# Layer 1 of a two-layer attention kernel: x1 loaded a second time in runs of 32 channels and turned by VectorE block transposes, in place of TensorE transposes

## The chip, the core and the metric

The kernel runs on one core of one Trainium2 chip. A core has five engines that run side by side and wait for each other through semaphores: TensorE (matrix products, PE in the profile; its weight loads are shown apart as PEld), VectorE (DVE), ScalarE (ACT), GpSimd (POOL) and SyncE (SP), which here only issues DMA transfers. Sixteen DMA engines move data between the device's main memory (HBM) and the core's on-chip memory (SBUF, 128 partitions). TensorE writes its results to PSUM, a small memory of its own, from which ScalarE and VectorE fetch them.

The metric is the device time of the whole program in microseconds (us), the median of several runs.

## What is computed

The input x has the shape (1, 128, 256, 256): 128 rows of 256 positions with 256 channels. Two layers follow each other. Each normalizes its input by groups of channels over the whole tensor, applies attention to every row of 256 positions, and adds the result to its input. Layer 0 has 8 heads, a bias from a pair tensor z and a gate. Layer 1, which the change concerns, has 4 heads of 64 channels and lets each position see only those at most 16 away. Cut to what matters:

```python
def _L1_conv_ref(x, w_in, b_in, w_out, b_out, band):
    x2 = x.reshape(B * T, F, C)
    qkv = x2 @ w_in.T + b_in
    q, k, v = jnp.split(qkv, 3, axis=-1)
    q, k, v = (heads(q), heads(k), heads(v))
    scores = jnp.einsum('bhid,bhjd->bhij', q, k) / jnp.sqrt(jnp.asarray(D, x.dtype))
    keep = jnp.abs(i - j) <= band
    scores = jnp.where(keep, scores, -jnp.inf)
    attn = jax.nn.softmax(scores, axis=-1)
    out = jnp.einsum('bhij,bhjd->bhid', attn, v)
    out = out.transpose(0, 2, 1, 3).reshape(B * T, F, C)
    return out @ w_out.T + b_out

x = x + _L0_conv_ref(_gn(x), ...)
x = x + _L1_conv_ref(_gn(x), ...)
```

All data is fp32.

## The kernel before

`fast_kernel` runs layer 0 over 64 pairs of rows and writes its result, x1, to HBM: sixteen tensors of 8 rows each (GB = 8, that is 4 pairs), stored when they are full (L1430). The sums for layer 1's normalization are collected along the way in `st1`. `general_kernel` stands behind a branch at the end and is taken only when a range check has failed.

**A pair in layer 1.** The class `Pair1` holds the work on two rows (512 positions). Its constructor allocates `xt` (positions on the partitions: 128 partitions, 4 blocks of positions, 256 channels; 4 buffers) and issues on SP the load of 512 KB from x1 (L1717), in contiguous runs of 1 KB. The projections need the channels on the partitions. So `transpose(k)`, for each half k of the channels, turns four blocks of 128x128 on TensorE into one PSUM buffer (L1730), and `centre(k)` moves that buffer to `xgT` on ScalarE, subtracting the channel's mean (L1733). After the second half GpSimd adds the output bias to `xt` in place (L1735), so that the residual needs one addition less later. `turn(k)` is the two together.

`project` makes q and k (four products a pair, evicted by ScalarE, L1747), `values` makes v (L1758, L1762), `scores` the products of q and k within the band (L1772), which ScalarE exponentiates (L1780) and GpSimd multiplies with a mask of the band in two instructions, e*bw (L1782). `apply` multiplies with v and sums the weights (L1800). `combine` brings the halves together on VectorE: sum (L1812), reciprocal (L1813), sum (L1814), product (L1816), and stores the reciprocals on SP (L1819). `out_row` projects back (L1831), VectorE adds `xt` (L1835, `yo`), and SP stores two rows (L1843).

**PSUM.** Transposes, projections, values and out_row take turns in two buffers named `mm`. A product can begin only when the one two places before it has been evicted. Scores, apply's results and its sums have buffers of their own, single ones.

**Order.** Within `manual_schedule` each engine's instructions follow the order of the program. The loop over p (L1884) is a pipeline over pairs: `now` does its scores and first apply, `was`, the pair before, its second apply and its output, `nxt` its projections, and `nn`, two pairs ahead, its load (at the top of the stage), and `turn(0)` and `turn(1)`. On TensorE the two groups of four transposes stand just ahead of `scores(1)` and, at the end of a stage, ahead of the next stage's `scores(0)`. On VectorE a stage has: `yo` of row 0, combine of row 1, combine of row 0, `yo` of row 1, and then, while there are any, one range check of three instructions (L958 to L960). There are 15 such checks, on `eb`, on the input mask and on sums read back from HBM; those of layer 0 come in stages 1 to 13, two more near the end.

**Entry.** Layer 1 begins with pairs 0 and 1: their loads, the transposes of pair 0 on TensorE, then `norm1`, which makes mean and scale from `st1` (VectorE L1682 copies the means, TensorE averages them, L1683 and L1691, VectorE and GpSimd follow) and multiplies the scale into `w_in` on VectorE (L1701). Then pair 0 is centred and projected, and pair 1 turned.

Of the kernel before, what the change touches and what calls it, by code (L numbers as in the profile page):

```python
# [9 lines left out]
F32 = mybir.dt.float32  # L10
AF = mybir.ActivationFunctionType
# [5 lines left out]
P = 128  # L17
# [4 lines left out]
def bcast(ap, axis, n):  # L22

    ap = ap.unsqueeze(axis)
    shape = list(ap.shape)
    shape[axis] = n
    return ap.broadcast_to(shape)
# [746 lines left out]
def fast_kernel(  # L774
# [25 lines left out]
    nc = tc.nc  # L800
    S, I, C = x.shape
# [6 lines left out]
    NB = I // P  # L808
    KC = C // P
    NP = S // 2  # L810
    N2 = 2 * I
# [7 lines left out]
    ident = const.tile([P, P], F32, name="ident")  # L819
# [89 lines left out]
    def rows(ap, s0, n):  # L909
        return ap[s0 : s0 + n].rearrange("s (b p) c -> p (s b) c", p=P)  # L910
# [20 lines left out]
    for a in range(KC):  # L931
        for h in range(H1):
            n = P // H1
# [5 lines left out]
    for h in range(H1):  # L939
        n = P // H1  # L940
# [257 lines left out]
    GB = min(8, S)  # L1198
    HQ = P // D0
    NT = 2 * NB  # L1200
    x1 = [dram.tile([GB, I, C], F32, name=f"x1_{j}") for j in range(S // GB)]
# [16 lines left out]
    class Pair:  # L1218


        def __init__(self, p):
            self.p = p
            self.oT = {}
            self.xt = la.tile([P, NT, C], F32, name="xt", tag="xt", bufs=5)
            nc.sync.dma_start(
                self.xt.rearrange("p (s b) c -> p s (b c)", b=NB),
                x[2 * p : 2 * p + 2].rearrange("s (p b) c -> p s (b c)", b=NB),
            )


        def centre(self):
            self.xg = la.tile([P, NT, C], F32, name="xg", tag="xg", bufs=2)
            nc.gpsimd.tensor_tensor(self.xg, self.xt, bcast(M0, 1, NT), ALU.subtract)
# [33 lines left out]
        def turn(self, pss=None):  # L1267
            self.xgT = la.tile([P, KC, N2], F32, name="xgT", tag="xgT", bufs=2)
            if pss is None:
                ps = ps_s.tile([P, KC, N2], F32, name="ps_x", tag="s")  # L1270
                pss = [ps[:, k, :] for k in range(KC)]
            for k in range(KC):
                for t in range(NT):
                    nc.tensor.transpose(  # L1274
                        pss[k][:, t * P : (t + 1) * P], self.xg[:, t, k * P : (k + 1) * P], ident
                    )
            for k in range(KC):
                nc.scalar.copy(self.xgT[:, k, :], pss[k])
# [201 lines left out]
    now = nxt = nn = None  # L1480
# [47 lines left out]
    behind, nx, n = None, 0, 0  # L1528
# [41 lines left out]
    with tc.manual_schedule():  # L1570
        old = was = Nobody()
        es = nn3 = None
        for p in range(NP):
# [49 lines left out]
            old, was, now, nxt, nn = was, now, nxt, nn, nn3  # L1623
# [21 lines left out]
    def q0(k):  # L1645
        return min(max(k * KB - BAND, 0), I - W)

    def half(k):
        return slice((k % 2) * KB, (k % 2 + 1) * KB)
# [9 lines left out]
            )  # L1659

    DH = P // H1
    LATE = 8
    rsum1 = dram.tile([NP, H1, 2, I], F32, name="rsum1")
    with tc.tile_pool(name="l1", bufs=2) as sb, tc.tile_pool(
        name="l1s", bufs=4
    ) as sm, tc.tile_pool(name="ps1_mm", bufs=2, space=PSUM) as ps_mm, tc.tile_pool(
        name="ps1_s", bufs=1, space=PSUM
    ) as ps_s, tc.tile_pool(name="ps1_o", bufs=1, space=PSUM) as ps_o:

        def mm1(name):  # L1670
            return ps_mm.tile([P, 512], F32, name=name, tag="mm")

        nM1 = const.tile([P, KC], F32, name="nM1")
# [36 lines left out]
        class Pair1:  # L1710


            def __init__(self, p):
                self.p = p
                s0 = 2 * p
                self.xt = sb.tile([P, 2 * NB, C], F32, name="xt1", tag="xt", bufs=4)
                nc.sync.dma_start(self.xt, rows(x1[s0 // GB], s0 % GB, 2))  # L1717
                self.es, self.oT = {}, {}

            def turn(self, k):  # L1720
                self.transpose(k)
                self.centre(k)

            def transpose(self, k):
                if k == 0:
                    self.xgT = sb.tile([P, KC, N2], F32, name="xgT1", tag="xgT")
                    self.ps_x = {}
                ps = self.ps_x[k] = mm1("ps_x1")
                for t in range(2 * NB):
                    nc.tensor.transpose(ps[:, t * P : (t + 1) * P], self.xt[:, t, k * P : (k + 1) * P], ident)  # L1730

            def centre(self, k):
                nc.scalar.activation(self.xgT[:, k, :], self.ps_x[k], AF.Identity, bias=nM1[:, k : k + 1])  # L1733
                if k == KC - 1:
                    nc.gpsimd.tensor_tensor(self.xt, self.xt, bcast(bout_r, 1, 2 * NB), ALU.add)  # L1735

# [50 lines left out]
            def apply(self, r):  # L1787
# [3 lines left out]
                for a in range(3):  # L1791
                    for j in range(NK // 2):
                        for h in range(H1):
                            for k in (2 * j, 2 * j + 1):
                                at = slice(h * DH, (h + 1) * DH)
                                n = k % 2
                                to = o_eo[n][at, a, q0(k) : q0(k) + W] if a < 2 else su_eo[n][at, q0(k) : q0(k) + W]
                                w = (self.v[half(k), r, j, h * D1 + a * DH : h * D1 + (a + 1) * DH] if a < 2
                                     else ones[half(k), :DH])
                                nc.tensor.matmul(  # L1800
# [3 lines left out]
            def combine(self, r):  # L1804
# [12 lines left out]
                self.oT[r] = oT  # L1817
                if r == 1 and self.p < NP - LATE:
                    nc.sync.dma_start(rsum1[self.p].rearrange("q r i -> q (r i)"), rv[0:P:DH].rearrange("q r i -> q (r i)"))  # L1819
                elif r == 1 and self.p < NP - 1:  # L1820
# [24 lines left out]
        def pair1(p):  # L1845
            return Pair1(p) if p < NP else Nobody()
# [5 lines left out]
        def check_all(src, lo, hi):  # L1852
            for i in range(0, src.shape[1], 512):
                n = min(512, src.shape[1] - i)
                checks.append(lambda i=i, n=n: check(src[:, i : i + n], lo, hi, sm))

        def load_sums(src, name):
            t = sb.tile([P, src.shape[0] // P], F32, name=name, tag=name, bufs=1)
            nc.sync.dma_start(t, src.rearrange("(a b) -> a b", a=P))
            check_all(t, 1e-16, 1e8)  # L1860

        with tc.manual_schedule():
            now, nxt = pair1(0), pair1(1)
            for k in range(KC):
                now.transpose(k)
            norm1()
            for k in range(KC):
                now.centre(k)
            for m in range(KC):
                now.project("qT", m)  # L1870
                now.project("kT", m)
            for r in range(2):
                now.values(r)
            for k in range(KC):
                nxt.turn(k)
        check_all(eb.rearrange("p h b i -> p (h b i)"), math.exp(-20.0), math.exp(20.0))
        mask_t = sb.tile([S, I], F32, name="mask_all", bufs=1)
        nc.sync.dma_start(mask_t, mask)
# [3 lines left out]
        with tc.manual_schedule():  # L1882
            was = Nobody()
            for p in range(NP - 1):  # L1884
                nn = pair1(p + 2)
                if p == NP - LATE + 2:
                    load_sums(rsum1[: NP - LATE].rearrange("n q r i -> (n q r i)"), "sums1")

                now.scores(0)
                was.apply(1)  # L1890
                was.out_row(0)
                was.combine(1)
                nxt.project("qT", 0)
                nxt.project("kT", 0)
                nxt.project("qT", 1)
                nn.turn(0)

                now.scores(1)
                now.apply(0)
                now.combine(0)  # L1900
                nxt.project("kT", 1)
                if p < NP - 2:
                    nxt.values(0)
                    nxt.values(1)
                was.out_row(1)
                nn.turn(1)
                if checks and p > 0:
                    checks.pop(0)()
                was, now, nxt = now, nxt, nn
            assert not checks  # L1910

            now.scores(0)
            was.apply(1)
            was.combine(1)
            now.values(0)
            was.out_row(0)
            now.scores(1)
            now.values(1)
            now.apply(0)
            now.combine(0)  # L1920
            was.out_row(1)
            now.apply(1)
            now.combine(1)
            now.out_row(0)
            now.out_row(1)
# [3 lines left out]
        ps = mm1("ok_ps")  # L1929
# [4 lines left out]
@with_exitstack  # L1934
def mixer_kernel(ctx, tc, *args):

    nc = tc.nc
    keep = ctx.enter_context(tc.tile_pool(name="verdict", bufs=1))
    verdict = keep.tile([1, 1], mybir.dt.int32, name="verdict")
    fast_kernel(tc, *args, verdict)  # L1940
    again = nc.values_load(verdict[0:1, 0:1], min_val=0, max_val=1)
    with tc.If(again > 0):
        general_kernel(tc, *args)
# [53 lines left out]
```

## Time and profile before

| What | Value |
|---|---|
| Median of 3 runs | 3363.17 us (3362.63 to 3363.67) |
| Profiled execution, from first to last instruction | 3356.3 us |
| Mean granted TensorE clock | 0.985 of full |
| Layer 1's transposes on TensorE (L1730) | 512, 128x128 fp32, busy 77.6 us |
| ScalarE centring (L1733) | 128, mean 683 ns |
| GpSimd bias addition (L1735) | 64, mean 2374 ns |
| VectorE `yo` (L1835) | 128, mean 690 ns |
| VectorE reciprocal of 128x256 (L1813) | 128, mean 1753 ns |
| DMA in layer 1, 2500 to 2600 us | engines busy 0.18 of the time, 55 GB/s |

The profile is of one execution, whose span is 3356.3 us; the runs' times are a few us longer because they count what lies around the first and last instruction too. Durations below are from that execution. The busy time of TensorE is modelled: its matrix instructions overlap, and a record's duration reaches from its start to the end of its pipeline. What an instruction really occupies is better read from start to start. Layer 1 begins at about 2095 us and lasts to the end.

### The profile page before, as it was taken

How to read it: one execution, taken by the hardware profiler on the slowest of the kernel's cores; microseconds unless marked ns; L12 is line 12 of the kernel's file. 1: busy time of each engine (PE TensorE's matmuls, PEld its weight loads, DVE VectorE, ACT ScalarE, POOL GpSimd, SP SyncE). 2: the span in 40 equal slices, each digit the busy share in tenths (PEclk: the TensorE clock that was granted, in tenths of full speed). 3: DMA queues.
4: the chain of work that ended last, by engine and by line, in shares of the span. 5: the costliest groups of instructions: out<-in, count | busy, mean ns of one | idle time of the engine just before them, and what ended most of it. 6: DMA issues, size and time to landing. Idle time of an engine off the chain costs nothing.

```text
span 3356.3 us, 81416 instructions
## 1 busy us (share of the span) xinstructions
PE 3210.8 (96%) x35168; PEld 2039.6 (61%) x35168; DVE 2021.7 (60%) x3115; ACT 1461.1 (44%) x2121; POOL 1961.9 (58%) x1375
## 2 busy tenths in 40 slices
PE   5389999999999999999999998999999999999998
PEld 3255555555555555555555555667777677677676
DVE  7955666666666666666666666466544444443456
ACT  2264444444444444444444443344444444444443
POOL 2378787777777787887777774333333333333332
PEclk8699999999999999999999999999999999999999
DMA  9941212221222222122212221111211211112111
GB/s 350 369 135 43 74 49 74 74 74 49 74 74 57 58 71 68 49 74 74 74 49 74 74 65 47 64 53 53 65 53 53 65 53 58 60 53 61 57 58 53
DMA packets 198640, 262.39 MB, mean 78 GB/s; under 512 B 46240, under 2 KB 147488, under 8 KB 197120
## 3 DMA queue, kind: packets, MB, share of 16 engines
q1 hardware_dynamic: 193200, 254.19, 24.7%
q8 instruction: 279, 4.57, 0.6%
q10 hardware_dynamic: 5072, 2.90, 0.3%
q14 instruction: 89, 0.73, 0.1%
HBM read 188.30 MB, written 68.75 MB: 77 GB/s over the span
## 4 chain that ended last, share of the span: by engine, by line
PE 91%; DVE 4%; DMA 3%; ACT 1%; POOL 1%; issue 1%; SPq 0%; ACTq 0%; POOLq 0%; DVEq 0%
PE ps_p L1296 20%; PE ps_p L1743 14%; PE ps_sc L1330 8%; PE ps_y L1831 7%; PE ps_ov L1362 7%; PE ps_v L1758 7%; PE ps_y L1417 6%; PE ps_v L1311 6%; PE ps_o L1800 3%; PE ps_sc L1772 3%; PE ps_su L1370 3%; PE ps_x L1274 2%; PE ps_x L1730 2%; PE ps_su L1800 1%; DVE st L1178 1%; DVE zst L1103 1%
## 5 line engine op out<-in xcount | busy, mean ns | idle before, releaser
L1351 POOL TENSOR_TENSOR eboth<-e 128x512 f32<-128x512 f32 x512 | 639.9, 1271 | 391.7 <-DVE e L1346 389.7
L1346 DVE TENSOR_TENSOR e<-ps_sc,eb 128x1024 f32<-128x1024 f32 x512 | 603.2, 1220 | 304.9 <-ACT ps_sc L1337 304.8
L1337 ACT ACTIVATE ps_sc<-ps_sc 128x1024 f32<-128x1024 f32 x512 | 492.8, 1006 | 509.2 <-PE ps_sc L1330 509.2
L1782 POOL TENSOR_TENSOR e<-e,bw 128x384 f32<-128x384 f32 x256 | 258.7, 1031 | 444.3 <-ACT e L1780 444.3
L1743 PE MATMUL ps_p<-xgT,w_in 128*128 128x512 f32 x1024 | 469.2, 601 | 3.7 <-DVE w_in L1701 3.7
L1735 POOL TENSOR_TENSOR xt<-xt,bout_r 128x1024 f32<-128x1024 f32 x64 | 152.0, 2374 | 379.0 <-PE ps_x L1730 379.0
L1835 DVE TENSOR_TENSOR yo<-ps_y,xt 128x512 f32<-128x512 f32 x128 | 88.3, 690 | 379.1 <-PE ps_y L1831 379.1
L1743 PEld LDWEIGHTS ps_p<-xgT,w_in 128*128 128x128 f32 x1024 | 188.9, 190 | 203.0 <-issue 170.9
L1330 PE MATMUL ps_sc<-qT,kT 32*128 32x256 f32 x4096 | 293.3, 400 | 2.0 <-ACT kT L1300 2.0
L1296 PE MATMUL ps_p<-xnT,wq 128*128 128x512 f32 x512 | 266.0, 631 | 3.5 <-POOL xnT L1283 2.9
L1831 PE MATMUL ps_y<-w_out,oT 128*128 128x256 f32 x1024 | 249.1, 386 | 2.6 <-DVE oT L1816 2.6
L1362 PE MATMUL ps_ov<-e,v 128*32 128x256 f32 x4096 | 247.7, 382 | 0.0
L1417 PEld LDWEIGHTS ps_y<-wo,oT 128*128 128x128 f32 x1024 | 194.3, 190 | 82.4 <-issue 59.3
L1417 PE MATMUL ps_y<-wo,oT 128*128 128x256 f32 x1024 | 242.0, 379 | 2.0 <-POOL oT L1407 1.2
L1330 PEld LDWEIGHTS ps_sc<-qT,kT 32*128 32x128 f32 x4096 | 184.9, 184 | 94.4 <-issue 83.6
L1311 PE MATMUL ps_v<-wv,xnT 128*128 128x256 f32 x1024 | 242.2, 379 | 0.0
L1296 PE MATMUL ps_p<-xnT,wk 128*128 128x512 f32 x512 | 240.6, 592 | 0.0
L1296 PE MATMUL ps_p<-xgT,wg 128*128 128x512 f32 x512 | 236.8, 605 | 0.0
L1758 PE MATMUL ps_v<-w_in,xgT 128*128 128x256 f32 x1024 | 231.8, 379 | 0.0
L1813 DVE RECIPROCAL rv<-odd 128x256 f32<-128x256 f32 x128 | 224.4, 1753 | 4.4
L1758 PEld LDWEIGHTS ps_v<-w_in,xgT 128*128 128x128 f32 x1024 | 194.4, 190 | 53.5 <-issue 30.1
L1311 PEld LDWEIGHTS ps_v<-wv,xnT 128*128 128x128 f32 x1024 | 189.6, 190 | 50.8 <-issue 31.0
(170 smaller groups left out, 4958.8 us busy)
## 6 DMA issues: line engine op xcount, KB each, us to landing
xa<-in_x_dram SPq DMA_DIRECT2D x8, 4096.0 KB
xt<-in_x_dram SPq DMA_DIRECT2D x64, 512.0 KB
x<-xo SPq DMA_DIRECT2D x16, 2048.0 KB
xt<-x SPq DMA_DIRECT2D x64, 512.0 KB
rvb<-rsum SPq DMA_DIRECT2D x252, 128.0 KB
out_dram<-yo SPq DMA_DIRECT2D x63, 512.0 KB
zt<-in_z_dram SPq DMA_DIRECT2D x15, 2048.0 KB
rs_r<-rs_d SPq DMA_DIRECT2D x63, 256.0 KB
```

What stands on the lines that cost most here:

```text
L1296: nc.tensor.matmul(ps, w[:, k, m * P : (m + 1) * P], getattr(self, src)[:, k, :], start=(k == 0), stop=(k == KC - 1),)
L1311: nc.tensor.matmul(self.ps_v[:, b * C : (b + 1) * C], self.xnT[:, k, t * P : (t + 1) * P], wv[:, k, :], start=(k == 0), stop=(k == KC - 1),)
L1330: nc.tensor.matmul(self.pss[q // 2][:, q % 2, b, :], self.kT[rs, c, r * I + b * P : r * I + (b + 1) * P], self.qT[rs, c, r * I : (r + 1) * I],
L1337: nc.scalar.activation(self.pss[a], self.pss[a], AF.Exp)
L1346: nc.vector.tensor_tensor(e, pss[a], eb[:, h : h + 2], ALU.mult)
L1351: nc.gpsimd.tensor_tensor(t, es[a][:, :, 0, :], es[a][:, :, 1, :], ALU.add)
L1362: nc.tensor.matmul(ov[q * D0 : (q + 1) * D0, c, :], self.v[:, r, b, h * D0 : (h + 1) * D0], es[q // 2][:, q % 2, b, :], start=(b == 0), st ...
L1417: nc.tensor.matmul(self.ps_y[:, b * C : (b + 1) * C], self.oT[r][:, k, b * P : (b + 1) * P], wo[:, k, :], start=(k == 0), stop=(k == KC - 1),)
L1743: nc.tensor.matmul(ps, w_in[:, k, n * C + m * P : n * C + (m + 1) * P], self.xgT[:, k, :], start=(k == 0), stop=(k == KC - 1),)
L1758: nc.tensor.matmul(ps[:, b * C : (b + 1) * C], self.xgT[:, k, t * P : (t + 1) * P], w_in[:, k, 2 * C : 3 * C], start=(k == 0), stop=(k == ...
L1782: nc.gpsimd.tensor_tensor(e[:, q], e[:, q], bcast(bw.rearrange("p b w -> p (b w)"), 1, KC), ALU.mult)
L1831: nc.tensor.matmul(ps[:, b * C : (b + 1) * C], self.oT[r][:, k, b * P : (b + 1) * P], w_out[:, k, :], start=(k == 0), stop=(k == KC - 1),)
```

## The change

Each pair is loaded twice. The old load into `xt` stays, for the residual, with 6 buffers instead of 4. A second load brings the same rows into `xs` (3 buffers) in four DMAs, one for each block j of 32 partitions: the partition of block j is the position within its run of 32 positions, and along the free dimension lie, for each half k of the channels and each run of 32 positions, 32 contiguous channels (128 bytes), channels k*128 + j*32 to k*128 + j*32 + 31. One VectorE instruction then transposes all 32x32 blocks of `xs` into `xT`, which has the channels on the partitions. `centre` reads `xT` instead of PSUM; `transpose` on TensorE is gone. The load now goes out three pairs ahead (`n3`), and `turn` stands at the end of a stage, after `yo` of row 1 and ahead of the range check; `centre(0)` and `centre(1)` of the pair after it stand where the two halves of `turn` stood. At the entry both pairs' `turn` stand ahead of `norm1`.

```diff
+    QB = 32
...
-                self.xt = sb.tile([P, 2 * NB, C], F32, name="xt1", tag="xt", bufs=4)
+                two = x1[s0 // GB][s0 % GB : s0 % GB + 2]
+                self.xs = sb.tile([P, KC, N2], F32, name="xs1", tag="xs", bufs=3)
+                for j in range(P // QB):
+                    nc.sync.dma_start(
+                        self.xs[j * QB : (j + 1) * QB].rearrange("b k (i a) -> b k i a", a=QB),
+                        two.rearrange("s (i b) (k j a) -> j b k (s i) a", b=QB, k=KC, a=QB)[j],
+                    )
+                self.xt = sb.tile([P, 2 * NB, C], F32, name="xt1", tag="xt", bufs=6)
                 nc.sync.dma_start(self.xt, rows(x1[s0 // GB], s0 % GB, 2))
                 self.es, self.oT = {}, {}
 
-            def turn(self, k):
-                self.transpose(k)
-                self.centre(k)
-
-            def transpose(self, k):
+            def turn(self):
+                self.xT = sb.tile([P, KC, N2], F32, name="xT1", tag="xT")
+                nc.vector.transpose(self.xT.rearrange("p k n -> p (k n)"), self.xs.rearrange("p k n -> p (k n)"))
+
+            def centre(self, k):
                 if k == 0:
                     self.xgT = sb.tile([P, KC, N2], F32, name="xgT1", tag="xgT")
-                    self.ps_x = {}
-                ps = self.ps_x[k] = mm1("ps_x1")
-                for t in range(2 * NB):
-                    nc.tensor.transpose(ps[:, t * P : (t + 1) * P], self.xt[:, t, k * P : (k + 1) * P], ident)
-
-            def centre(self, k):
-                nc.scalar.activation(self.xgT[:, k, :], self.ps_x[k], AF.Identity, bias=nM1[:, k : k + 1])
+                nc.scalar.activation(self.xgT[:, k, :], self.xT[:, k, :], AF.Identity, bias=nM1[:, k : k + 1])
                 if k == KC - 1:
                     nc.gpsimd.tensor_tensor(self.xt, self.xt, bcast(bout_r, 1, 2 * NB), ALU.add)
...
             now, nxt = pair1(0), pair1(1)
-            for k in range(KC):
-                now.transpose(k)
+            now.turn()
+            nxt.turn()
             norm1()
...
             for k in range(KC):
-                nxt.turn(k)
+                nxt.centre(k)
...
             for p in range(NP - 1):
-                nn = pair1(p + 2)
+                nn = pair1(p + 2) if p == 0 else n3
+                n3 = pair1(p + 3)
+                if p == 0:
+                    nn.turn()
...
                 nxt.project("qT", 1)
-                nn.turn(0)
+                nn.centre(0)
...
                 was.out_row(1)
-                nn.turn(1)
+                nn.centre(1)
+                n3.turn()
                 if checks and p > 0:
                     checks.pop(0)()
```

## The prediction

> **What bounds the kernel now.** I read the page's busy shares first, then layer 1 in the chain of waits, then one steady pair in the timeline, then the places where the change adds something: VectorE beside the checks, the entry into layer 1, and the DMA of short runs.
>
> The page: TensorE is the only engine near its limit.
>
> ```profile
> PE 3210.8 (96%) x35168; PEld 2039.6 (61%) x35168; DVE 2021.7 (60%) x3115; ACT 1461.1 (44%) x2121; POOL 1961.9 (58%) x1375
> ...
> PE 91%; DVE 4%; DMA 3%; ACT 1%; POOL 1%; issue 1%; SPq 0%; ACTq 0%; POOLq 0%; DVEq 0%
> ```
>
> The chain within layer 1 (start us, us, what): one pair every 2622.98 - 2603.71 = 19.27 us, TensorE without a hole, and the transposes (ps_x) in it.
>
> ```profile
> 2603.71 5.15 PE ps_p L1743 x12
> 2608.86 0.44 PE ps_x L1730 x4
> 2609.30 0.82 PE ps_sc L1772 x32
> ...
> 2622.98 2.15 PE ps_p L1743 x5
> ```
>
> The timeline of that pair (start us, us, engine, line, what, and the idle time before it) shows both groups of four transposes with their neighbours, and what VectorE does from one eviction `yo` to the next: nothing, for 3.84 us.
>
> ```profile
> 2608.70 0.60 PE L1730 MATMUL ps_x<-ident,xt 128*128 128x128 f32 x4
> 2609.22 0.70 PEld L1772 LDWEIGHTS ps_sc<-qT,kT 64*64 64x64 f32 x32 [0.17 <-issue]
> 2618.34 0.60 PE L1730 MATMUL ps_x<-ident,xt 128*128 128x128 f32 x4
> 2618.54 0.69 DVE L1835 TENSOR_TENSOR yo<-ps_y,xt 128x512 f32<-128x512 f32 x1 [3.21 <-PE ps_y L1831]
> 2618.87 0.89 PE L1772 MATMUL ps_sc<-qT,kT 64*64 64x96 f32 x32
> 2623.07 0.69 DVE L1835 TENSOR_TENSOR yo<-ps_y,xt 128x512 f32<-128x512 f32 x1 [3.84 <-PE ps_y L1831]
> ```
>
> In 15 of the pairs a range check (L958 has 8 on eb, 1 on the mask, 6 on sums) fills just that gap. It delays the second `yo` so far that the weight load of the next projection waits for it; there the period is 19.30 us (2218.04 to 2237.34 in the chain), so the gap is used up to within 0.03 us.
>
> ```profile
> 2174.99 0.69 DVE L1835 TENSOR_TENSOR yo<-ps_y,xt 128x512 f32<-128x512 f32 x1 [3.21 <-PE ps_y L1831]
> 2175.47 2.38 POOL L1735 TENSOR_TENSOR xt<-xt,bout_r 128x1024 f32<-128x1024 f32 x1 [5.93 <-PE ps_x L1730]
> 2175.60 2.54 DVE L958 TENSOR_SCALAR chk<-eb 128x512 f32<-128x512 f32 x1
> 2178.17 1.37 DVE L959 SCALAR_TENSOR_TENSOR chk<-eb,chk 128x512 f32<-128x512 f32 x1
> 2180.18 0.68 DVE L1835 TENSOR_TENSOR yo<-ps_y,xt 128x512 f32<-128x512 f32 x1
> 2180.91 0.30 PEld L1743 LDWEIGHTS ps_p<-xgT,w_in 128*128 128x128 f32 x2 [0.59 <-DVE yo L1835]
> ```
>
> The entry into layer 1: SP and VectorE are both let go by the last store of layer 0 at 2095.4; TensorE, in order, first waits for xt and transposes it, and only then does the mean (L1683), whose input is ready at 2095.8.
>
> ```profile
> 2095.44 0.93 SPq L1717 DMA_DIRECT2D xt<-x  x2
> 2095.48 0.29 DVE L1682 COPY gn_each<-st 128x256 f32<-128x256 f32 x1 [2.92 <-DMA x<-xo]
> 2099.54 1.94 PE L1730 MATMUL ps_x<-ident,xt 128*128 128x128 f32 x8 [11.98 <-issue]
> 2101.27 1.06 PE L1683 MATMUL ps_gn<-gn_each,avg 128*128 128x256 f32 x2
> ```
>
> **What the Trainium skill says.** "VectorE: DVE Perf Modes", The three transpose paths: VectorE turns 32x32 blocks only, which is why the load must place the blocks; no run shows it yet. "DMA: Bandwidth & Descriptors", Specifications: transfers under 512 B miss line rate; the new runs have 128 B. The trace agrees in direction only: 1 KB packets take about 51 ns (DMA view from 2600 to 2640 us: 2311 packets in 18.4% of 16 engines), while the 4-byte packets of `rs_d` take some 11 ns each (DMA view from 1016 to 1020 us: 512 packets, 32 an engine, within about 0.4 us). "SBUF — State Buffer", Who interferes with whom: VectorE and GpSimd share a port pair as an exclusive lock, taken by tensor_scalar and by instructions with two SBUF inputs. The trace agrees: L958 takes 2.54 us and ends just after POOL L1735, but 0.42 us in the same shape (`chk<-rv`) with GpSimd idle.
>
> **The change part by part.**
>
> Removed on TensorE. Start to start, the transposes hold it from 2608.70 to 2609.23 and from 2618.34 to 2618.87: 0.53 us twice, 1.06 us a pair. (The chain, which counts by ends, gives 0.44 twice; that is the lower bound.) Pairs 1 to 63 have them in the stream: 63 x 1.06 = 66.8 us. Pair 0 belongs to the entry, below. What is late next: nothing. With the transposes gone the two PSUM buffers `mm` rotate over eight users instead of ten, still even, and apply, out_row and project keep their 2 to 8 us of distance from what VectorE and ScalarE deliver.
>
> Added on VectorE: one transpose of 128x1024 per pair. The trace has none. Nearest row: tensor_tensor of 128x1024 (L1346) at 1.22 us, and "Vector Engine (DVE) Microarchitecture Reference", The reshape front-end and per-opcode configuration, states one element per cycle per lane. I take 1.22. Lower bound 0.7 (two per cycle); upper bound the rate of the reciprocal, 1753 ns for 256, that is 7.0 us. It stands right behind the second row's `yo`, with behind it in the queue (checks aside) the other row's `yo`. That one is wanted 0.53 us earlier than before: 4.53 - 0.53 = 4.0 us after the first, and the projection tolerates about 0.63 more. 0.61 + 1.22 = 1.83 fits: cost nothing, up to a transpose of 4.0 us.
>
> With a check behind it. Transpose ends at 1.83; GpSimd no longer waits for TensorE with the bias add (it moves forward behind the e*bw products, and may hold up one L1816 by 0.8 us, which has 5 us), but its two e*bw products of 0.98 us then begin at about 1.7. L958 waits for the first (to 2.7), L959 for the second, and `yo` starts at about 5.0 against a limit of 4.63: 0.37 us lost. If L958 comes first, nothing is lost; if the check costs its full 4.6 us, 1.8 us. I take 0.35 x 15 = 5 us, range 0 to 27.
>
> ScalarE reads xT in SBUF instead of PSUM: same count, 0.68 us each, with the input two stages old; no cost.
>
> DMA. Per pair four loads of 32 partitions, each 32 x 32 runs of 128 B: 4096 runs, 256 an engine when the 32 partitions spread over 16. From 11 ns at 4 B and 51 at 1 KB a straight line gives 16 ns at 128 B: 4.1 us a pair. Bounds: 11 ns, and 40 ns should a short run cost nearly what a long one does. SP issues four more DMAs at about 0.46 us (1.8 us). They come first in a stage; behind them on SP stand xt, the store of the sums and of the rows, none of them urgent. The load has from there to the end of the same stage, 18.2 us: 0.5 + 1.8 + 4.1 + about 2 to land = 8.4. Hidden, up to about 60 ns a run. If it is not there, VectorE stands at the transpose, and behind it the next `yo`, which TensorE needs to go on. The xt load, now one stage earlier with six buffers, is off the path.
>
> Entry. Both transposes stand on VectorE ahead of gn_each. SP starts at 2095.44, data some 0.9 us later; xs, xt, xs in turn take 4.1 + 1.6 + 4.1 = 9.8 us, 1 us to land, then 1.22 and 0.3: L1683 at about 2108.7 instead of 2101.27: +7 us (11 ns: +5; 40 ns: +20). The 1.94 us of TensorE transposes are in that difference.
>
> Sum: -66.8 + 5 + 7 = -54.8 us on a span of 3356.3. The execution has 6.9 us around its span against the median of 3363.17; I leave them as they are: 3308 us.
>
> **Rivals.**
> A. Cover too thin: the transpose takes 2.5 to 4 us, or every check costs the full stall, with loads at 40 ns. -66.8 + 27 + 20 = -20: 3343. For it: the gap in checked pairs was used up to 0.03 us. Against: 15 of 64 pairs only.
> B. Slower: the load of short runs becomes the bound. SP issues a pair's load after the previous stage's store, and VectorE waits for it before the next `yo`; beyond about 60 ns a run each pair lasts as long as its load. At 80 ns: 256 x 0.08 + 3.3 (xt and store) = 23.8 us instead of 19.27, 62 x 4.5 = +280: 3640. For it: the skill's warning about short transfers, and no such read in the trace. Against: the 4-byte packets at 11 ns, and DMA at 0.2 of its time.
> C. The transpose runs at the reciprocal's rate, 7.0 us: 0.61 + 7.0 - 4.63 = 3.0 us lost in each pair against 1.06 won: 62 x 1.94 + 5 + 7 + 27 = about +160: 3523. It decides from 5.1 us up. Against: it computes nothing.
>
> **Numbers.** Forecast 0.72, A 0.15, B 0.08, C 0.03; 0.02 for a change without effect, some stall that I don't see giving the gain back. 0.2% is 6.7 us, about what can be told from no change. Faster 0.72 + 0.15 = 0.87, same 0.02, slower 0.08 + 0.03 = 0.11. The range: best case -66.8 with no check stall and +5 at the entry, 3301; less a little for what I can't see, 3297. Upward it takes in rival A: 3345.
>
> **What would show it.** Right: no PE ps_x in layer 1, the chain's period at about 18.2 us, the transposes at about 1.2 us with VectorE idle behind them, checked pairs longer by 0.3 to 0.5 us, the mean L1683 at 7 us after its old place. Wrong: VectorE's transposes waiting for the xs load in every stage (B), transposes above 4 us with PE ps_p waiting for `yo` (C), or a period that stays near 19.

## The result, and the profile after

| | Before | After |
|---|---|---|
| Median | 3362.9 us (3362.45 to 3363.67, 4 runs) | 3314.69 us (3310.73 to 3316.03, 4 runs) |
| Ratio, 95% interval | | 0.9855 [0.9841, 0.9869] |
| Span of the profiled execution | 3356.3 us | 3314.3 us |
| Period of a pair without a check | 19.27 us | 18.39 us |
| Period of a pair with a check | 19.30 us | 18.39 us |
| Last store of layer 0 to layer 1's first projection | 20.2 us | 27.7 us |
| Last store of layer 0 to the first product of layer 1's first values | 29.0 us | 38.4 us |

The period is the time from a pair's first projection to the next pair's. The gain is 48.2 us where 54.8 were forecast. The first two lines of the page of the kernel after, busy shares and the chain by engine, show the same picture as before: TensorE has lost its 512 transposes and is still the only engine near its limit.

```profile
PE 3157.9 (95%) x34656; PEld 1977.2 (60%) x34656; DVE 2121.6 (64%) x3179; ACT 1452.7 (44%) x2121; POOL 1962.8 (59%) x1375
...
PE 91%; DVE 3%; DMA 3%; ACT 1%; POOL 1%; SPq 1%; issue 0%; ACTq 0%; POOLq 0%; DVEq 0%
```

The chain of waits of the kernel after, over one steady pair (start us, us, what). It is TensorE alone, nothing stands between the projections and the scores any more, and from one group of twelve projections to the next pass 2611.34 - 2592.95 = 18.39 us.

```profile
2592.95 5.15 PE ps_p L1745 x12
2598.10 0.82 PE ps_sc L1774 x32
...
2605.58 1.73 PE ps_y L1833 x8
2607.31 0.82 PE ps_sc L1774 x32
...
2611.34 3.00 PE ps_p L1745 x7
```

The timeline of the same pair. The block transpose takes 1.24 us right behind the first `yo`; VectorE is then idle for 2.25 us ahead of the second, and the cover is not used up. GpSimd's bias addition now runs while VectorE makes the first row's `oT`, which takes 1.59 us instead of 0.69.

```profile
2602.13 2.36 POOL L1737 TENSOR_TENSOR xt<-xt,bout_r 128x1024 f32<-128x1024 f32 x1
2603.45 1.59 DVE L1818 TENSOR_TENSOR oT<-odd,rv 128x512 f32<-128x512 f32 x1
...
2607.34 0.69 DVE L1837 TENSOR_TENSOR yo<-ps_y,xt 128x512 f32<-128x512 f32 x1 [2.31 <-PE ps_y L1833]
2607.95 1.24 DVE L1730 STREAM_TRANSPOSE xT<-xs 128x1024 f32<-128x1024 f32 x1
2611.44 0.69 DVE L1837 TENSOR_TENSOR yo<-ps_y,xt 128x512 f32<-128x512 f32 x1 [2.25 <-POOL e L1784]
```

A pair with a range check, same view. L958 comes ahead of GpSimd's products by 0.06 us and takes 0.38 us, where the kernel before needed 2.54. The second `yo` begins 2188.49 - 2184.30 = 4.19 us after the first, within the 4.63 that the prediction allowed.

```profile
2184.30 0.69 DVE L1837 TENSOR_TENSOR yo<-ps_y,xt 128x512 f32<-128x512 f32 x1 [2.31 <-PE ps_y L1833]
2184.91 1.23 DVE L1730 STREAM_TRANSPOSE xT<-xs 128x1024 f32<-128x1024 f32 x1
2186.06 0.38 DVE L958 TENSOR_SCALAR chk<-eb 128x512 f32<-128x512 f32 x1
2186.12 2.60 POOL L1784 TENSOR_TENSOR e<-e,bw 128x384 f32<-128x384 f32 x2 [4.67 <-ACT e L1782]
2186.48 1.37 DVE L959 SCALAR_TENSOR_TENSOR chk<-eb,chk 128x512 f32<-128x512 f32 x1
...
2188.49 0.68 DVE L1837 TENSOR_TENSOR yo<-ps_y,xt 128x512 f32<-128x512 f32 x1
```

The entry into layer 1, same view. VectorE stands at the two turns until their loads have landed; the mean follows 2111.64 - 2098.41 = 13.23 us after SP was let go. Then comes something that the prediction has no term for: the scaling of `w_in` takes 5.83 us, beside two bias additions on GpSimd, and TensorE stands once more between the first two products of the projections and the third.

```profile
2098.41 2.90 SPq L1720 DMA_DIRECT2D xs<-x  x4
...
2104.80 1.25 DVE L1730 STREAM_TRANSPOSE xT<-xs 128x1024 f32<-128x1024 f32 x1 [9.28 <-DMA xs<-x]
...
2110.02 1.25 DVE L1730 STREAM_TRANSPOSE xT<-xs 128x1024 f32<-128x1024 f32 x1 [3.98 <-DMA xs<-x]
...
2111.64 1.19 PE L1684 MATMUL ps_gn<-gn_each,avg 128*128 128x256 f32 x2 [21.14 <-issue]
...
2116.38 4.69 POOL L1737 TENSOR_TENSOR xt<-xt,bout_r 128x1024 f32<-128x1024 f32 x2
2116.44 5.83 DVE L1702 TENSOR_SCALAR w_in<-w_in,gn_R 128x256 f32<-128x256 f32 x6 [0.90 <-POOL gn_R L1697]
...
2118.97 2.05 PE L1745 MATMUL ps_p<-xgT,w_in 128*128 128x512 f32 x2 [3.69 <-issue]
...
2121.36 8.47 PE L1745 MATMUL ps_p<-xgT,w_in 128*128 128x512 f32 x14 [0.35 <-DVE w_in L1702]
```

In the kernel before only one addition fell beside the scaling, and TensorE went through without a stop:

```profile
2105.93 3.74 DVE L1701 TENSOR_SCALAR w_in<-w_in,gn_R 128x256 f32<-128x256 f32 x6 [0.90 <-POOL gn_R L1696]
...
2108.51 9.00 PE L1743 MATMUL ps_p<-xgT,w_in 128*128 128x512 f32 x16 [3.74 <-DVE w_in L1701]
```

One by one, the first scaling takes 2.43 us in the kernel before and the first two 2.43 us each in the kernel after, while an addition runs on GpSimd; the others take 0.34. The trace also shows TensorE's granted clock at about half here (0.53 from 2091 to 2113 us before, 0.50 from 2095 to 2126 us after), with a product starting every 0.85 us instead of every 0.43. It is back at full 3.8 us after the first product in the kernel before and 6.9 us after it in the kernel after. So the entry loses 27.7 - 20.2 = 7.5 us up to the first projection and 38.4 - 29.0 = 9.4 us up to the values.

The account: 63 pairs x (19.27 - 18.39) = -55.4 us; entry +9.4; checks 15 x -0.03 = -0.4. Together -46 us, against 48.2 [44.0, 53.5] measured. The two spans differ by only 42.0, because in this execution of the kernel after layer 0, which the change doesn't touch, ended 2.95 us later; it was 2.9 us behind already at 292 us, and from 215 to 275 us its granted clock was 0.91 where the kernel before had 0.97. Executions of the kernel after lie up to 5.3 us apart, so a difference of 2 us is not explained here.

### The profile page after: what moved, and what is told of

Its sections match the earlier page's. It is cut to its first block, busy times and chain, and to the rows that moved or that the text cites. A ratio compares the mean times of both kernels' runs of the same rounds, so it can differ in the third digit from the quotient of the medians.

```text
span 3314.3 us, 80768 instructions
## 1 busy us (share of the span) xinstructions
PE 3157.9 (95%) x34656; PEld 1977.2 (60%) x34656; DVE 2121.6 (64%) x3179; ACT 1452.7 (44%) x2121; POOL 1962.8 (59%) x1375
## 4 chain that ended last, share of the span: by engine, by line
PE 91%; DVE 3%; DMA 3%; ACT 1%; POOL 1%; SPq 1%; issue 0%; ACTq 0%; POOLq 0%; DVEq 0%
PE ps_p L1296 21%; PE ps_p L1745 14%; PE ps_sc L1330 8%; PE ps_y L1833 7%; PE ps_ov L1362 7%; PE ps_v L1760 7%; PE ps_y L1417 7%; PE ps_v L1311 6%; PE ps_o L1802 3%; PE ps_su L1370 3%; PE ps_sc L1774 3%; PE ps_x L1274 2%; PE ps_su L1802 1%; DVE st L1178 1%; DVE zst L1103 1%; DMA zt<-in_z_dram 1%
## 5 line engine op out<-in xcount | busy, mean ns | idle before, releaser
L1760 PEld LDWEIGHTS ps_v<-w_in,xgT 128*128 128x128 f32 x1024 | 194.4, 190 | 53.5 <-issue 30.1
L1317 DVE TENSOR_TENSOR v<-ps_v,vb_r 128x512 f32<-128x512 f32 x128 | 88.6, 692 | 206.8 <-PE ps_v L1311 206.8
```

What stands on the lines that cost most here:

```text
L1760: nc.tensor.matmul(ps[:, b * C : (b + 1) * C], self.xgT[:, k, t * P : (t + 1) * P], w_in[:, k, 2 * C : 3 * C], start=(k == 0), stop=(k == ...
```

## The experiments

All of them start from the kernel after; line numbers are each kernel's own.

**The price of a transpose.** The prediction read 0.53 us per group of four from start to start, which I had called the better reading; the chain of the kernel before, by ends, had 0.44. Four transposes, or one, go back in ahead of each `scores`, into a part of the scores' PSUM buffer that is free; their results are not used.

```diff
                 at = lambda q, c, j: ps[:, q, (c * 2 + j) * W : (c * 2 + j + 1) * W]
+                for t in range(4):      # one_back: range(1)
+                    nc.tensor.transpose(ps[:, t % 2, 384:512], self.xt[:, t, 0:P], ident)
```

> The changed kernel with four TensorE transposes put back ahead of every scores; their results go to unused columns of the scores' own PSUM buffer and are not used. If a group costs what the chain of before says, 0.44 us, the period goes from 18.39 to 19.27 us, that of the kernel before, and the total to about 3370 us. If it costs 0.53 us, as counted from start to start: 19.45 us, about 3381 us.

> The same with one transpose ahead of every scores in place of four; its result is not used. Theory (changeover): scores that follow wide products directly lose about 0.09 us in changing over, and a transpose in between takes that loss on itself, so four cost 4 x 0.1325 - 0.09 = 0.44 us and one costs 0.04: period 18.47 us. Rival (each costs 0.11 us, alike): 18.61 us.

four_back took 3365.89 us and one_back 3325.11 (the kernel before beside them 3363.25; one run each). The chain of four_back:

```profile
2417.05 5.15 PE ps_p L1745 x12
2422.20 0.44 PE ps_sc L1771 x4
2422.64 0.82 PE ps_sc L1776 x32
...
2436.34 3.86 PE ps_p L1745 x9
```

and of one_back:

```profile
2408.96 5.15 PE ps_p L1745 x12
2414.11 0.11 PE ps_sc L1771
2414.22 0.82 PE ps_sc L1776 x32
...
2427.57 2.58 PE ps_p L1745 x6
```

The period is 19.29 with four and 18.61 with one, against 18.39 with none: 0.45 for a group of four, 0.11 for a single one, so each costs 0.11 and there is no fixed part. The theory of a cost at each changeover to and from transposes falls. With four put back the period is that of the kernel before again, 19.29 us against 19.27, although the second load, the deeper buffers and VectorE's transpose are still there: what the steady pair gained is the transposes' time on TensorE. Where the other 0.1 of the start-to-start reading lies, the starts show. One transpose and the scores behind it, in the timeline of one_back:

```profile
2413.94 0.27 PE L1771 MATMUL ps_sc<-ident,xt 128*128 128x128 f32 x1
2414.15 0.89 PE L1776 MATMUL ps_sc<-qT,kT 64*64 64x96 f32 x32
```

From start to start this is 0.21 us, and 0.53 to 0.54 with four: 0.11 for each transpose and 0.10 that belongs to none. With no transpose the scores still begin about 0.1 us after the projections' last step (twelve steps of 0.43 us from 2592.79 end at 2597.95; the scores begin at 2598.03). That pause was there before, hidden in the pitch that I gave to the transposes.

**The entry.** Three kernels. In norm_split the mean and scale go ahead of the turns, the scaling behind the first, and the second pair's turn behind the centring:

```diff
             now, nxt = pair1(0), pair1(1)
+            R1c = norm1()
             now.turn()
-            nxt.turn()
-            norm1()
+            scale1(R1c)
             for k in range(KC):
                 now.centre(k)
+            nxt.turn()
```

> Only the entry into layer 1 differs from the changed kernel: norm1's averages come first, then pair 0's block transpose, then the six scalings of w_in, then pair 1's block transpose. Theory 1 (order of VectorE's queue): in the changed kernel the mean waited 13.2 us from SP's release because two loads and two transposes stood ahead of it. Here the mean starts about 0.5 us after the release, the first projection about 10 us after it instead of 20.6, and the total falls by 9 to 12 us, to about 3304 us. Rival (the entry is bound by the loads themselves and by a cold TensorE, wherever norm1 stands): at most 2 us less, about 3313 us. The steady period stays 18.39 us under both.

It measured 3300.14 us (3299.14 to 3302.47, 5 runs) against 3360.45 of the kernel before, 0.9823 [0.9809, 0.9836]: a gain of 60.3 us, 12.1 more than the change alone. Its timeline at the entry:

```profile
2094.93 2.80 SPq L1723 DMA_DIRECT2D xs<-x  x4
...
2095.47 1.19 PE L1684 MATMUL ps_gn<-gn_each,avg 128*128 128x256 f32 x2 [8.44 <-DMA x<-xo]
...
2100.90 1.25 DVE L1733 STREAM_TRANSPOSE xT<-xs 128x1024 f32<-128x1024 f32 x1 [1.53 <-DMA xs<-x]
2102.07 3.71 DVE L1705 TENSOR_SCALAR w_in<-w_in,gn_R 128x256 f32<-128x256 f32 x6
...
2103.15 7.31 PE L1748 MATMUL ps_p<-xgT,w_in 128*128 128x512 f32 x10 [4.05 <-DVE w_in L1705]
```

The mean runs 0.5 us after SP's release while the loads are under way, and the projections begin after 8.2 us, where the kernel after has 2118.97 - 2098.41 = 20.6. That is 12.3 us; counted from layer 0's last store to the first product of the values it is 13.3 (25.1 us instead of 38.4). Either agrees with the 12.1 of the total within the spread: the entry lost by the two turns standing ahead of a step that needs nothing from them. With that mended the values begin 3.9 us sooner than in the kernel before (29.0), which itself had a load and transposes ahead of the mean.

In bias_later both bias additions of the entry wait until the end of the first stage:

```diff
-            def centre(self, k):
+            def centre(self, k, add=True):
...
-                if k == KC - 1:
+                if k == KC - 1 and add:
...
-                now.centre(k)
+                now.centre(k, False)
...
-                nxt.centre(k)
+                nxt.centre(k, False)
...
                 n3.turn()
+                if p == 0:
+                    now.add_bias()
+                    nxt.add_bias()
```

> Only GpSimd's bias additions of pairs 0 and 1 move: from the entry to the end of the first stage. Theory (port lock): the six scalings of w_in take 5.83 us in the changed kernel against 3.74 before because the second bias addition, which no longer waits for TensorE's transposes, runs beside them; here they take about 3.7 us and the total falls by about 2 us, to 3312.6. Rival (the scalings are slow for another reason, the loads for one): they stay at 5.8 us and the total at 3314.7.

Measured: 3310.76 us (3309.6 to 3311.69, 4 runs), 0.9853 [0.9838, 0.9868]. The gain, 49.7 us, can't be told from the 48.2 of the change. Its timeline tells more:

```profile
2113.80 1.66 DVE L1702 TENSOR_SCALAR w_in<-w_in,gn_R 128x256 f32<-128x256 f32 x6 [0.90 <-POOL gn_R L1697]
```

With GpSimd idle the scaling takes 1.66 us, less even than the 3.74 of the kernel before, which had one bias addition beside it; the expectation of 3.7 overlooked that both additions move. From SP's release to the first projection pass 18.3 us instead of 20.6, and to the first product of the values 28.1 instead of 31.3. So the two additions cost the entry 2.3 to 3.1 us, of which the kernel before paid a part too, for one; it is shown in the trace and lost in the spread of the totals.

both_entry makes both edits.

```diff
+            R1c = norm1()
             now.turn()
-            nxt.turn()
-            norm1()
+            scale1(R1c)
             for k in range(KC):
-                now.centre(k)
+                now.centre(k, False)
+            nxt.turn()
```

> Both entry edits together: norm1's averages ahead of the block transposes, and the two bias additions at the end of the first stage. If the two losses are separate they add up: the first projection about 8.5 to 9 us after SP's release, total 3301 to 3303 us. If the one hides behind the other: no better than the better of the two alone.

3299.41 us (3298.1 to 3303.68, 5 runs), 0.9823 [0.981, 0.9837]: no better than norm_split. The two losses don't add. In norm_split the first addition has to wait for its own load of `xt` and runs from 2102.99 us, so that it holds up only the fifth of the six scalings (2103.08 to 2105.52 us), which belongs to v, and the values don't begin before 2112.88. From the last store to there it is 25.1 us in norm_split and 25.6 in both_entry. norm_split is the version to keep.

**VectorE's cover.** The turn is made three times.

```diff
-                nc.vector.transpose(self.xT.rearrange(...), self.xs.rearrange(...))
+                for _ in range(3):
+                    nc.vector.transpose(self.xT.rearrange(...), self.xs.rearrange(...))
```

> The changed kernel with the block transpose done three times over (the same result each time): VectorE's gap takes 0.61 + 3 x 1.235 = 4.3 us. Theory (the limit is about 4.5 us behind the first yo, when the weight load of the second projection begins to wait): pairs without a check keep 18.39 us, pairs with one get longer by about 2 us (4.3 + 1.8 to 2.4 for the check, against 4.5). Rival (any more work in the gap delays the next yo and the delay reaches TensorE): pairs without a check longer by 0.4 us or more.

3339.54 us (one run). A pair without a check keeps 18.39 us although VectorE has 2.5 us more to do. A pair with one takes 19.75 (2163.47 to 2183.23 to 2202.98 in the timeline):

```profile
2170.67 0.69 DVE L1838 TENSOR_TENSOR yo<-ps_y,xt 128x512 f32<-128x512 f32 x1 [2.30 <-PE ps_y L1834]
2171.28 3.79 DVE L1731 STREAM_TRANSPOSE xT<-xs 128x1024 f32<-128x1024 f32 x3
...
2175.00 0.39 DVE L958 TENSOR_SCALAR chk<-eb 128x512 f32<-128x512 f32 x1
2175.42 0.69 DVE L959 SCALAR_TENSOR_TENSOR chk<-eb,chk 128x512 f32<-128x512 f32 x1
...
2176.75 0.68 DVE L1838 TENSOR_TENSOR yo<-ps_y,xt 128x512 f32<-128x512 f32 x1
...
2177.48 3.70 PE L1746 MATMUL ps_p<-xgT,w_in 128*128 128x512 f32 x8 [1.09 <-DVE yo L1838]
```

Now TensorE waits for `yo`. It begins 6.08 us after the first, 1.45 beyond the 4.63 of the prediction, and the pair lasts 1.36 longer: the tolerance is measured at 6.08 - 1.36 = 4.72 us. Adding the 2.47 us of two transposes to the 4.19 of the kernel after would give 2.0; the check gives 0.6 back, because GpSimd is done by then and L959 takes 0.69 instead of 1.37. The trace as a whole fits: from layer 0's last store to the end it takes 1244.3 us against 1223.0, 21.3 us more, where the longer pairs with a check make 19.4 and the entry, up to the values, 2.5.

**The load.** Each short-run DMA is issued four times, the copies into tiles that nothing reads.

```diff
+                xd = [sb.tile([P, KC, N2], F32, name=f"xd{n}", tag=f"xd{n}", bufs=2) for n in range(3)]
...
-                    nc.sync.dma_start(self.xs[...], two[...])
+                    for dst in [self.xs] + xd:
+                        nc.sync.dma_start(dst[...], two[...])
```

> The changed kernel with every load of short runs issued four times, three of them into tiles that nobody reads: sixteen DMAs of 1024 runs a pair in place of four. Theory (SP's issue): an issue takes about 1.1 us for 1024 runs, so SP needs 16 x 1.1 + 1.5 = 19 us or more for a pair, more than the 18.39 of TensorE: period 19.2 to 19.7 us, VectorE waiting for the load. Rival (the DMA engines are what counts, 13 ns a run): 16 x 64 x 13 ns = 13.3 us and 3.3 us for xt and the store, 16.6 us in all, hidden: period 18.39 us.

3468.55 us and a period of 20.54, beyond what any of my theories gave, and not for their reasons. The chain:

```profile
2500.88 1.73 PE ps_p L1747 x4
...
2502.64 0.70 ACT qT L1751
...
2503.38 2.00 PE ps_p L1747 x4
```

Each projection waits until ScalarE has evicted the one before it. The reason that I take, from the addresses in the built program, which no view here shows, is that the two `mm` buffers are no longer handed out in turn and all four projections of a pair lie in the same one. The edit had moved a decision that it does not mention, so the run doesn't say what the load costs. I gave the buffers out strictly in turn, which ends these waits, and repeated it with four and with two issues:

```diff
+        turns = []
...
         def mm1(name):
-            return ps_mm.tile([P, 512], F32, name=name, tag="mm")
+            turns.append(name)
+            return ps_mm.tile([P, 512], F32, name=name, tag=f"mm{len(turns) % 2}", bufs=1)
...
+                xd = [... for n in range(3)]   # loads_x2_alt: range(1)
```

> The kernel after, with each of the four short-run DMAs of a pair issued four times (three copies go to tiles that nothing reads), and with the two PSUM buffers mm given out strictly in turn. In loads_x4 the period of a pair was 20.54 us, and TensorE stood 0.78 and 0.84 us ahead of its second and third projection, each time until ScalarE had evicted the one before: there the building program had put all four projections of a pair into one PSUM buffer, so that the run measured this besides the loads. Theory 1 (SP): an issue of 1024 short runs holds SP about 1.05 us, so sixteen of them with the other three issues of a stage take 18.9 to 19.5 us, more than the 18.39 of the pair: period 18.9 to 19.5, SP's queue without idle time, TensorE waiting for it once a pair. Theory 2 (all of the loss in loads_x4 came from the PSUM buffer): period 18.39. Theory 3 (the DMA engines: 1024 runs each of them at 13 ns, 13.3 us, and 3.6 us for the rest, less than a period): hidden, as theory 2; but at 20 ns a run under load 24 us, and VectorE would wait for xs in every stage.

> As loads_x4_alt with each short-run DMA issued twice. SP needs 8 x 1.05 and about 2.1 for the rest, 10.5 us of the 18.39; the DMA engines 512 runs at 13 ns, 6.7 us, and 3.6 us for the rest. Both theories of the load: period 18.39, total within 5 us of the kernel after apart from the entry, where two pairs' second loads delay the normalization by about 10 us. A rival that says the load is only just hidden now: a period above 18.6.

loads_x2_alt: 3324.25 us, period 18.43 on average. Twice the load is hidden; of the 8.2 us that it is longer than the profiled execution of the kernel after, 7.4 are the later mean at the entry. loads_x4_alt: 3435.7 us, period 20.0 on average (from 2610.48 to 2949.90 us, 17 pairs), but uneven, with pairs from 18.4 to 24.7 us. VectorE's timeline there:

```profile
2526.88 0.69 DVE L1842 TENSOR_TENSOR yo<-ps_y,xt 128x512 f32<-128x512 f32 x1 [2.31 <-PE ps_y L1838]
2531.08 1.25 DVE L1735 STREAM_TRANSPOSE xT<-xs 128x1024 f32<-128x1024 f32 x1 [3.51 <-DMA xs<-x]
2532.25 0.65 DVE L1842 TENSOR_TENSOR yo<-ps_y,xt 128x512 f32<-128x512 f32 x1
```

This is the prediction's rival B: VectorE stands at the turn until the load lands, and the next `yo` behind it is late. SP's queue has no gap in it. But does SP set the pace, or do the DMA engines, which let its queue drain? Two more runs, with the transfers of loads_x4_alt. In loads_x4_two six of the twelve copies are issued on ScalarE's queue, one after each eviction of projections and values; in loads_x4_long the copies are made in runs of 1 KB.

```diff
 loads_x4_two
+                        if (n == 1 or n == 3 and j < 2) and p > 5:
+                            later.append((to, at))
+                        else:
+                            nc.sync.dma_start(to, at)
 ...
+                nc.scalar.dma_start(*later.pop(0))
 loads_x4_long
+                            dst[j * QB : (j + 1) * QB].rearrange("b k (h c) -> b (k h) c", c=C),
+                            two.rearrange("s (i b) c -> b (s i) c", b=P)[j * QB : (j + 1) * QB],
```

> loads_x4_alt with six of the twelve needless short-run DMAs of a pair issued on ScalarE's queue, one after each of its six evictions of projections and values, from pair 6 on; the transfers are the same. loads_x4_alt took 20.0 us a pair, its SP queue without a gap, and the loads came late. Open is what held SP: its own work on each issue, or the DMA engines, which let an issue through only as fast as they move the runs. Theory 1 (SP's own work): SP has ten issues of about 1.05 us and 2.1 us for the rest, 12.6 us of the 18.39, and the period falls to 18.4 to 18.9, above 18.39 only for what ScalarE loses by its six issues. Theory 2 (the DMA engines are full at 4096 x 4 short runs a pair, about (20.0 - 3.3) / 1024 = 16 ns a run): period 20.0 or more, and issues on both queues drawn out.

> loads_x4_alt with the twelve needless DMAs of a pair in runs of 1 KB in place of 128 bytes: the same bytes and the same number of issues, 1536 runs in place of 12288. Theory 1a (SP pays for each DMA, about 1.05 us whatever its runs): period 20.0 as in loads_x4_alt. Theory 1b (SP pays by the run) and theory 2 (the DMA engines pay by the run: 256 x 16 ns + (64 + 96) x 51 ns = 12.3 us): period 18.4, with SP's issues of the long runs at 0.3 to 0.6 us.

loads_x4_two: 3478.4 us, period 20.7 on average. loads_x4_long: 3331.99 us, period 18.44. Issues in the timeline of loads_x4_two, where those on ScalarE take 0.56 us (563 ns at least, 564 in the median of 348, 2893 at most), and some on SP far more:

```profile
2512.47 0.56 ACTq L1675 DMA_DIRECT2D xd<-x  x1
...
2515.95 3.54 SPq L1734 DMA_DIRECT2D xd<-x  x2
```

and in loads_x4_long, where three issues of long runs take 0.54 each:

```profile
2519.57 1.61 SPq L1729 DMA_DIRECT2D xd<-x  x3
```

The same number of issues of the same bytes is hidden when the runs are long, so a DMA has no fixed price that matters; and taking six issues off SP doesn't help. The share of time for which the 16 DMA engines are busy points the same way. From 2300 to 2500 us it is 0.38 in the kernel after and 0.67 with two issues, 1.07 with four and 1.17 with four on two queues (packets overlap, so that their times can add up to more than 1). With the long runs it is 0.95 and just hidden, at 173 GB/s where loads_x4_alt moves 160: it isn't the bytes. An issue of 1024 short runs itself holds its engine for 0.56 us; what SP shows above that is probably its queue waiting to drain. So the DMA engines' time for the runs is the likely bound: (20.0 - 3.3) / 1024 = 16 ns a run, with the prediction's 3.3 us for `xt` and the store. It isn't isolated strictly. In loads_x4_two SP also waited 54 us in a window of 200 for landings of earlier copies, a wait that the second queue brought in. And theory 2 had expected drawn-out issues on both queues, where ScalarE's stayed at 0.56 us.

## Why the prediction was right

The forecast was 3308 us, between 3297 and 3345; 3314.69 were measured. Term by term:

- **TensorE, 1.06 us a pair: mis-sized, 0.88 measured.** This term carries the miss: 63 x 0.18 = 11.4 us of gain that wasn't there. I took the pitch of the starts and called the chain's 0.44 a lower bound; it was the price. four_back and one_back show 0.11 for each transpose, and the pause of 0.1 ahead of the scores is not the transposes'. The period came to 18.39 us, not the 18.2 named as a sign. That nothing is late next held: TensorE has no hole in the steady pair.
- **VectorE, 1.22 us for the block transpose.** 1.235 in the median of 64. The tolerance of 4.63 us was 4.72 (turn_x3).
- **Checks, 5 us: mis-sized, none.** Their period is 18.39 us, that of the others. Of the three cases it was the one called "L958 comes first, nothing is lost"; it came first by 0.06 us. That was luck: in the case it counted on, `yo` at 5.0 us, the measured tolerance of 4.72 would have let about 0.28 us a pair be lost, an estimate from turn_x3, or 4 us in all.
- **ScalarE.** 0.717 us from SBUF instead of 0.683 from PSUM, 128 times, beside TensorE: no cost, as said.
- **The bias addition moves forward.** It holds up one L1818 by 0.9 us (0.8 foreseen), harmless in a pair. At the entry the same move did cost: the second addition, which had waited for TensorE's transposes, now fell beside the scaling of `w_in` like the first. That is the lock that the Trainium skill's "SBUF — State Buffer", Who interferes with whom, describes for VectorE and GpSimd; the six scalings took 1.66, 3.74 and 5.83 us with no, one and two additions beside them, one scaling of 2.43 us for each addition. The prediction used the lock for L958, and didn't ask at the entry which instructions the moved addition would meet.
- **DMA, 16 ns a run, hidden.** The load never held VectorE in the steady pairs. 128-byte packets took 13 ns in the median; the bound in loads_x4_alt gives 16. That agrees with the Trainium skill's "DMA: Bandwidth & Descriptors", Specifications, on short transfers: 128 bytes in 16 ns are 8 bytes a ns, 1 KB in 51 ns 20. SP's 0.46 us an issue was too low (0.56 when the queue is free, 1.1 on average), with no effect.
- **Entry, +7 us: mis-sized, +9.4.** The mean came 13.23 us after the release, 13.3 foreseen, and up to the first projection the loss was 7.5. The other 1.9 us came after it, and the prediction has no term for them: a stop of TensorE of about 0.6 us ahead of the third product (it starts 1.41 us after the second, the others 0.85), until the scaling held up by the second addition was done, and a granted clock that stayed at half for longer, 6.9 us beyond the first product instead of 3.8. The clock isn't the addition's doing alone: in bias_later, with none there, it was 5.8 us.
- **The rivals.** A and C didn't occur. B's mechanism is real, at the place it named: with four times the runs, equal to 64 ns each in its sum, its formula with the prediction's own 16 ns a run gives 1024 x 0.016 + 3.3 = 19.7 us, and loads_x4_alt took 20.0. The change itself stays well clear, since twice the load is still hidden.

The terms that were off, +11.4 on TensorE, -5 at the checks and +2.4 at the entry, come to 9 us less gain than forecast; 6.6 were measured, within the spread of the executions. In the steady pairs TensorE alone sets the time and no load is waited for, as forecast. That the total came so near is in part luck: a stall that didn't happen made up for almost half of what TensorE's term promised too much.

## What to carry to other kernels

What a removed instruction gives back is the difference of two periods; ahead of the run, read it from the chain by ends, since the pitch of the starts can hold a pause that stays. When a step leaves an in-order engine, look at the first iteration as well as the steady one: here 12 of 60 us lay in two instructions that waited for a load ahead of a step that didn't need it. In an experiment that adds tiles or transfers, compare which buffers the rest of the kernel was given before reading its time.

## What the runs showed of the hardware

- A VectorE transpose of all 32x32 blocks in 128x1024 fp32 takes 1.235 us, as long as an addition of that shape (1.22).
- An fp32 transpose of 128x128 on TensorE occupies it for 0.11 us in the stream, though its record alone shows 0.27.
- An issue of 1024 runs of 128 bytes holds an engine's queue for 0.56 us at least, which on ScalarE's queue was the median too; on SP's, behind other loads, it took up to 4.6 us (loads_x4_alt).
- Sixteen such issues a pair, 16384 runs, don't fit into 18.39 us (20.0 on average); the same bytes with three quarters of them in runs of 1 KB do (18.44).
- A multiplication of `w_in`, 128x256, takes 0.34 us on VectorE with GpSimd idle and 2.43 us behind a GpSimd addition of 128x1024 (2.34 to 2.39 us): it waits until the addition is done.
- At the entry, after TensorE had stood waiting, its granted clock was half; projections started every 0.85 us there and every 0.43 us in the steady pairs. It was back at full 3.8 to 6.9 us after the first of them (before and after).
